# Mixed convolution weights and context terms: one product each, handed out by transfers through DRAM

## The chip, the cores and the metric

The kernel runs on one core of a Trainium2 chip. The metric is the device time of one execution in microseconds (us). An execution is timed as a whole; one execution was also recorded by the hardware profiler, and every row below is from that one.

## What is computed

Four layers follow one another on x of (32 batches, 64 channels, 1024). Each is x = x + FFN(cond(x)). Two kinds of conditioning matter here:

```python
# layers 0 and 3: a 1x1 convolution whose weights are mixed per batch
att   = softmax(mlp(cond))                          # (32, 8)
agg_w = einsum('bk,koi->boi', att, weight[..., 0])  # (32, 64, 64)
agg_b = att @ bias_k                                # (32, 64)
out   = einsum('boi,bih->boh', agg_w, x) + agg_b[:, :, None]

# layers 1 and 2: a grouped convolution, 9 taps, with a context term
out = conv(x, weight, groups=4)                     # (32, 64, 1024)
ctx = einsum('nd,od->no', cond, c_weight)           # (32, 64)
out = out + ctx[:, :, None] + fside[None, :, None]
```

The FFNs: layer 0 a top-1 mixture of LoRA experts, layer 1 a linear layer with weights and activations rounded to 8-bit integers and a separate part for outlier columns, layer 2 a linear layer plus top-2 LoRA experts, layer 3 a squared-relu FFN plus a latent expert and a layer norm.

## The kernel before

**Tiles.** x is kept on the chip as 16 tiles `x[j]` of 128 partitions: two batches of 64 channels, 1024 columns. So a mixed weight for tile j is a 128 x 128 matrix `aw[:, j, :]` with the 64 x 64 matrices of the tile's two batches on its diagonal and zeros elsewhere, and a context term for tile j is 2 x 64 numbers that every one of the 128 partitions needs.

**The mixing, for layers 0 and 3.** `fetch3` (L191) loads the eight weight matrices in four row groups. `mixing` (L195) clears `aw` on GpSimd (POOL), then makes 256 small products on TensorE (PE), L206: for each of 64 output channels, in four parts, and for both batches of a tile, an 8 x 64 slice of the weights is stationary and the 8 x 16 attention columns of all tiles move. VectorE (DVE) evicts with L212. Layer 0 does that at the start; layer 3's mixing stands in layer 2's loop, after tile 3's iteration (`if j == 4`, L802), and is stored to DRAM (`awd`) in two transfers; layer 3 loads four tiles' part at a time (`aw0` at L829 for the first, L865 for the later ones).

**The context, for layers 1 and 2.** `context` (L176) is called for each tile: POOL multiplies c_weight by the tile's two cond columns (`cpr`, L179), PE sums over partitions with a matrix of ones (`cb`, L186), and DVE adds `fside` (`cbs`, L188). `conv` (L233) then makes 32 products (L239) and DVE's eviction (L242) adds the context.

**Layer 0's loop** (L371 to L404) runs 16 + 5 iterations; in iteration `it` it loads two tiles ahead (`load`, L277: xT and x, on SyncE's queue, SP), a piece of layer 1's weight (`wt`), projects tile `it` (`z`, L286), makes the context of tile it-4, routes tile it-1 (`route0`: `lh`, L293 and L294, with the mixed weight `aw`), turns and multiplies tile it-2 (`whT` L316, `o` L325), and does layer 1's convolution of tile it-5 (`conv1`). When tile j's row is done, `by_rows` (L226) copies it from `x[j]` to `g`, rearranged for the convolution, in eight transfers on SP (L230); `g` has two buffers. Between these stand the steps of layer 1's weight quantization: its largest absolute values (`scb`, L342 and L344 on DVE, L396 on POOL with an all-reduce), the reciprocals (`top`, L399 to L401 on DVE) and the products (`wq`, L348 on POOL). After the loop, layer 1's `keep` (L408) starts; `bins<-zero` (L412) clears 8 MB of DRAM for layer 2's routing.

**Layer 2's first loop** runs over the 16 tiles: `features2` (context, convolution), `by_rows` two tiles ahead, half of an earlier tile's base product (`base2`, `o`, L681, stored by `x<-xo`, L689), `route2` (`lr`, L622), `place2` (`rk`, L653 and L654), and side work of layer 3's weights (`raw`, `ds`).

**Order.** Each engine runs its instructions in one order, fixed when the program is built: a scheduler orders each engine's instructions by its own estimate of when they can start, so the order differs from the text of the loops. SP, ACT and POOL issue transfers from their own queues; a transfer that waits holds back those behind it in its queue. Eight completion semaphores are shared by the transfers of SP and ACT, eight by POOL's: a transfer also waits for the one that used its semaphore last. Small row tiles (`tag="row"`) have 8 buffers, shared by contexts, biases and others.

## Time and profile before

| | us |
|---|---|
| runs, fastest, median, slowest of 3 | 1797.51, 1806.03, 1808.48 |
| profiled execution, its own time | 1798.23 |
| its span, first to last instruction | 1796.3 |

The mean TensorE clock granted in that execution is 0.984 of full speed. The span cuts into stretches at the places where the layers meet, with PE's busy time and DMA's mean share:

| stretch, us | what | PE busy | DMA share |
|---|---|---|---|
| 0 to 195.1 | layer 0 and layer 1's convolution | 163.4 | 0.75 |
| 195.1 to 365.7 | layer 1's FFN | 160.7 | 0.27 |
| 365.7 to 585 | layer 2, first loop | 212.6 | 0.56 |
| 585 to 763 | layer 2, experts | 171.3 | 0.81 |
| 763 to 1796.3 | layer 3 | 1015.4 | 0.57 |

How to read the rows. The page's first block gives each engine's busy time, share of the span and number of instructions. The chain is the work that ended last, followed back from the last instruction; its shares say where time, if taken away, would have to come from. A timeline row has the start, the duration, the engine, the line, the operation, destination<-source by the program's names, the shape, the count, and in brackets the idle time ahead of it and what ended that. In the table of stretches a row has the stretch, its length, and for PE, PEld, DVE, ACT and POOL the busy time with the number of instructions, then PE's granted clock, the DMA share and GB/s. A matrix product in f32 takes two passes and is counted as two instructions.

### The profile page before, as it was taken

To read this page: it belongs to the slowest core of one execution; us is meant where nothing else is said; L and a number is where in the kernel's file an instruction comes from. 1 tells how busy PE (TensorE), PEld (TensorE's weight loads), DVE (VectorE), ACT (ScalarE), POOL (GpSimd) and SP (SyncE) were. 2 spreads that over 40 slices of the span, in tenths; PEclk is the share of its full clock that TensorE was granted. 3 is DMA by queue.
4 is the path that set the end of the run, shared out by engine and by line. 5 is a ranking of instruction groups with operands and counts; after the bars stand their busy time and mean duration, and the time that the engine had idled before them with its cause. 6 is when DMAs were issued, how large, how long until landed. Compare 5 with 4: busy or idle time off the path is not lost.

```text
span 1796.3 us, 20943 instructions
## 1 busy us (share of the span) xinstructions
PE 1723.4 (96%) x7526; PEld 1157.7 (64%) x7526; DVE 811.5 (45%) x1700; ACT 203.4 (11%) x547; POOL 607.1 (34%) x628
## 2 busy tenths in 40 slices
PE   7987899999999999999999999999999999999997
PEld 6876577666766434486486585585584775774863
DVE  2889799455654433364152531143520333611224
ACT  1000344100000032010000010000010000000000
POOL 2347255522432564224044142052331242420231
PEclk9988899999999999999999999999999999999999
DMA  6886331277651499794576465475655574744423
GB/s 237 240 249 157 94 83 63 87 193 205 183 146 47 169 367 367 275 313 164 183 274 246 165 213 179 158 287 182 218 180 170 205 281 146 241 153 147 152 88 111
DMA packets 187351, 342.06 MB, mean 190 GB/s; under 512 B 20592, under 2 KB 93056, under 8 KB 187248
## 3 DMA queue, kind: packets, MB, share of 16 engines
q1 hardware_dynamic: 173152, 297.33, 51.2%
q0 software_dynamic: 14096, 43.39, 7.0%
q8 instruction: 60, 0.98, 0.2%
q14 instruction: 43, 0.35, 0.1%
HBM read 239.85 MB, written 83.89 MB: 180 GB/s over the span
## 4 chain that ended last, share of the span: by engine, by line
PE 79%; DMA 7%; POOL 4%; issue 4%; DVE 4%; SPq 2%; ACT 0%; POOLq 0%; DVEq 0%
PE p_d L1030 26%; PE p_u L975 25%; PE o L681 9%; PE conv L239 5%; PE oo L461 3%; DMA m<-outs,slot 2%; PE lr L622 2%; PE fold L263 1%; PE mix L565 1%; DMA bg<-in_b_dram,ewi 1%; POOL bin L537 1%; POOL x L470 1%; SPq L230 1%; DMA x<-in_x_dram 1%; POOL lo L454 1%
## 5 line engine op out<-in xcount | busy, mean ns | idle before, releaser
L1030 PE MATMUL p_d<-dn,h 128*128 128x512 f32 x1120 | 483.6, 593 | 0.0
L1030 PEld LDWEIGHTS p_d<-dn,h 128*128 128x128 f32 x1120 | 212.4, 190 | 263.9 <-issue 261.6
L975 PE MATMUL p_u<-y,up 128*128 128x256 f32 x1680 | 364.8, 379 | 0.5 <-DVE v_u L932 0.5
L975 PEld LDWEIGHTS p_u<-y,up 128*128 128x128 f32 x1680 | 318.8, 190 | 46.3 <-issue 2.1
L681 PE MATMUL o<-base,yT 128*128 128x512 f32 x512 | 225.1, 595 | 0.5 <-DVE eo L768 0.5
L681 PEld LDWEIGHTS o<-base,yT 128*128 128x128 f32 x512 | 95.3, 190 | 117.5 <-issue 113.8
L239 PE MATMUL conv<-cw,g 128*128 128x128 f32 x1024 | 126.0, 284 | 0.0
L239 PEld LDWEIGHTS conv<-cw,g 128*128 128x128 f32 x1024 | 123.6, 201 | 0.2
L461 PE MATMUL oo<-cbt,lo 128*128 128x512 f32 x256 | 104.2, 407 | 5.8 <-POOL lo L454 3.8
L461 PE MATMUL oo<-cbt,hi 128*128 128x512 f32 x256 | 104.7, 409 | 0.0
L988 POOL TENSOR_TENSOR raw<-u_u,v_u 128x256 f32<-128x256 f32 x40 | 30.2, 755 | 216.0 <-DVE v_u L932 215.9
L1003 POOL TENSOR_TENSOR h<-h 128x256 f32<-128x256 f32 x40 | 34.7, 869 | 148.4 <-DVE h L997 113.3
L687 DVE TENSOR_TENSOR xo<-x,o 128x256 f32<-128x256 f32 x64 | 35.4, 594 | 107.8 <-PE o L681 102.0
L932 DVE TENSOR_TENSOR v_d<-e_d,p_d 128x512 f32<-128x512 f32 x16 | 11.0, 687 | 143.4 <-PE p_d L1030 143.4
L975 PE MATMUL p_u<-y,s 128*128 128x256 f32 x320 | 72.2, 379 | 0.0
L932 DVE TENSOR_TENSOR v_u<-e_u,p_u 128x256 f32<-128x256 f32 x40 | 16.8, 420 | 111.5 <-PE p_u L975 111.5
L617 POOL TENSOR_TENSOR x<-x,bias 128x512 f32<-128x512 f32 x32 | 37.0, 1176 | 87.3 <-DMA g<-x 84.3
L975 PEld LDWEIGHTS p_u<-y,s 128*128 128x128 f32 x320 | 60.8, 190 | 8.3
L926 DVE TENSOR_TENSOR u_d<-e_d,p_d 128x512 f32<-128x512 f32 x16 | 11.0, 688 | 118.4 <-PE p_d L1030 118.4
L548 DVE TENSOR_TENSOR m<-m,m 128x1024 f32<-128x1024 f32 x32 | 42.4, 1326 | 45.2 <-DMA m<-outs,slot 23.0
L461 PEld LDWEIGHTS oo<-cbt,lo 128*128 128x128 f32 x256 | 49.0, 191 | 21.3 <-POOL lo L454 8.3
L975 PE MATMUL p_u<-y,r 128*128 128x256 f32 x240 | 57.7, 389 | 3.9 <-DVE v_u L932 2.8
(243 smaller groups left out, 2113.0 us busy)
## 6 DMA issues: line engine op xcount, KB each, us to landing
dn<-ds SPq DMA_DIRECT2D x160, 256.0 KB, 3.5
up<-us SPq DMA_DIRECT2D x60, 512.0 KB, 4.7
outs<-eo SPq DMA_DIRECT2D x48, 512.0 KB, 6.5
dn<-in_dn_dram SPq DMA_DIRECT2D x96, 256.0 KB, 3.5
g<-x SPq DMA_DIRECT2D x256, 64.5 KB, 2.5
up<-in_up_dram SPq DMA_DIRECT2D x30, 512.0 KB, 3.7
ds<-sum SPq DMA_DIRECT2D x20, 512.0 KB, 3.6
us<-s SPq DMA_DIRECT2D x20, 512.0 KB, 3.1
```

The costliest lines, as they stand in the source:

```text
L239: nc.tensor.matmul(ps[:, g, :], rows[:, 4 * b + g, ds(w, P)], cwt[:, g, w, :], start=(w == 0), stop=(w == 1))
L461: nc.tensor.matmul(po, terms[j][i][:, c, :], cbt[c][:, ts(n, HF)], start=(c == 0 and i == 0), stop=(c == NC - 1 and i == 1),)
L548: nc.vector.tensor_tensor(got[0], got[0], got[1 + k], ALU.add)
L617: nc.gpsimd.tensor_tensor(xh(j, h), xh(j, h), halved(bias2[:, ts(h, HF)]), ALU.add)
L622: nc.tensor.matmul(ps, yT[j][:, c, :], ra2[:, c, :], start=(c == 0), stop=(c == NC - 1))
L681: nc.tensor.matmul(po, yT[j][:, c, :], base[c][:, ts(n, HF)], start=(c == 0), stop=(c == NC - 1))
L687: nc.vector.tensor_tensor(new, old[:, ts(n, 64), :], add, ALU.add)
L932: nc.vector.tensor_tensor(m["v"], m["e5"], m["7"], ALU.add)
L975: nc.tensor.matmul(ps[0], ws[i][:, k, c, :], y[RHS[p]][:, c, :], start=(start and c == 0), stop=(c == 3), skip_group_check=not start,)
L988: nc.gpsimd.tensor_tensor(raw[:, 1, 1], m["u"], m["v"], ALU.add)
L1003: tt(h[:, 4], h[:, 1], h[:, 3], ALU.add)
L1030: nc.tensor.matmul(ps[q], hs[k][:, HLHS[p], ts(q, P)], ws[k], start=(start and k == 0), stop=(k == HG - 1), skip_group_check=not start,)
```

## The change

- `context`'s products are replaced by `contexts(n)`: one product of cond (stationary, all 32 batches) with c_weight for each of layers 1 and 2, `fside` added, stored to DRAM (`ctxd`). `context(n, j)` is now one SP transfer that loads tile j's 2 x 64 numbers to all 128 partitions.
- `mixing` is replaced by `aggregate(n)`: the attention is stationary in a 32 x 32 tile of the array, four such tiles on the diagonal hold the four row groups, and each takes 512 columns at a time: 8 products for a layer (16 in PE's passes). DVE evicts one half, ScalarE (ACT) the other, and ACT's queue stores the 32 mixed 64 x 64 matrices to DRAM (`aggd`) in four transfers of 128 KB. `spread` loads them back into the diagonal blocks of `aw`, which POOL has cleared, with two transfers of 256-byte runs: layer 0 all 16 tiles at once on ACT's queue, layer 3 four tiles at a time on SP's.
- Both layers' `aggregate` and both `contexts` stand at the start of layer 0. Layer 2's loop loses its mixing, and layer 3 keeps one cleared `aw3` for its later batches.
- Layer 0 loads three tiles ahead instead of two and projects one tile earlier; `z0` has 4 buffers instead of 3.
- Layer 0's order on SP changes with that: the loads of tiles 0 to 10 and six `wt` loads stand before the first `by_rows`, and `bins<-zero` stands ahead of the `by_rows` of tiles 7 and 8, where it stood after that of tile 9.
- The host lays the mixed weights out with the input channel first.

```diff
@@ -168,48 +168,47 @@
             nc.vector.tensor_copy(atT, ps)
             att[n] = atT
 
-    def context_weights(n, pool):
-        cw = pool.tile([P, 64], F32, name=f"ctxw{n}")
+    ctxd = {n: dram.tile([NB, 64], F32, name=f"ctxd_{n}") for n in (1, 2)}
+    aggd = {n: dram.tile([NB, 64, 64], F32, name=f"aggd_{n}") for n in (0, 3)}
+
+    def contexts(n, tmp):
+
+        cw = tmp(f"ctxw_{n}")[:, 0:64]
         nc.gpsimd.dma_start(out=cw, in_=a[f"cwT_{n}"])
-        return cw
-
-    def context(n, j, cw):
-
-        pr = small.tile([P, 2, 64], F32, tag="row", bufs=8, name=f"cpr{n}_{j}")
-        nc.gpsimd.tensor_tensor(
-            pr,
-            cw[:, None, :].to_broadcast([P, 2, 64]),
-            condT[:, ts(j, 2), None].to_broadcast([P, 2, 64]),
-            ALU.mult,
-        )
-        ps = bank(f"cb{n}_{j}", (P, 2, 64))
-        nc.tensor.matmul(ps, ones, pr, start=True, stop=True)
+        ps = bank(f"ctx_{n}", (NB, 64))
+        nc.tensor.matmul(ps, condT, cw, start=True, stop=True)
+        t = tmp(f"ctxs_{n}")[:NB, 0:64]
+        nc.vector.tensor_tensor(t, ps, fside[:NB], ALU.add)
+        nc.gpsimd.dma_start(out=ctxd[n], in_=t)
+
+    def context(n, j):
         cb = small.tile([P, 2, 64], F32, tag="row", bufs=8, name=f"cbs{n}_{j}")
-        nc.vector.tensor_tensor(cb, ps, fside[:, None, :].to_broadcast([P, 2, 64]), ALU.add)
+        nc.sync.dma_start(out=cb, in_=ctxd[n][ts(j, 2)].partition_broadcast(P))
         return cb
 
-    def fetch3(n, w3):
+    def aggregate(n, w3, t, evicts):
+
         for r in range(4):
             nc.gpsimd.dma_start(out=w3[ds(32 * r, KC)], in_=a[f"w3_{n}"][r])
-
-    def mixing(n, aw, w3, evict):
-
-        for t in aw:
-            nc.gpsimd.memset(t, 0.0)
-        w = w3.rearrange("k (o i) -> k o i", i=64)
-        at = att[n].rearrange("k (j h) -> k h j", h=2)
-        ps = [bank(f"awp_{n}_{r}", (P, 16, NT)) for r in range(4)]
-        for o in range(16):
+        ps = [bank(f"agg_{n}_{c}") for c in range(2)]
+        for c in range(2):
             for r in range(4):
-                q = ds(32 * r, KC)
-                for h in range(2):
-                    nc.tensor.matmul(ps[r][ds(64 * h, 64), o, :], w[q, o, :], at[q, h, :], start=True, stop=True)
+                q = ds(32 * r, 32)
+                k = ds(32 * r, KC)
+                nc.tensor.matmul(ps[c][q], att[n][k], w3[k, ts(c, HF)], start=True, stop=True)
+        for c in range(2):
+            evicts[c](t[:, ts(c, HF)], ps[c])
         for r in range(4):
-            for h in range(2):
-                q = ds(64 * h, 64)
-                m = NT // len(aw)
-                for i, t in enumerate(aw):
-                    evict(t[q, :, ds(64 * h + 16 * r, 16)], ps[r][q][:, :, ts(i, m)].rearrange("p o j -> p j o"))
+            nc.scalar.dma_start(
+                out=aggd[n][:, ts(r, 16), :].rearrange("b i o -> b (i o)"), in_=t[ds(32 * r, 32)]
+            )
+
+    def spread(n, aw, j0, eng):
+
+        src = aggd[n].rearrange("(j h) i o -> h i j o", h=2)
+        for h in range(2):
+            q = ds(64 * h, 64)
+            eng.dma_start(out=aw[q, :, q], in_=src[h, :, ds(j0, aw.shape[1]), :])
 
     def mixed_bias(n, j, bk, eng):
 
@@ -284,7 +283,7 @@
                 ps = bank(f"z0_{j}", (P, E0 + P))
                 for c in range(NC):
                     nc.tensor.matmul(ps, xT[:, c, :], ra[:, c, :], start=(c == 0), stop=(c == NC - 1))
-                z = lp.tile([P, E0 + P], F32, tag="z0", bufs=3, name=f"z0s_{j}")
+                z = lp.tile([P, E0 + P], F32, tag="z0", bufs=4, name=f"z0s_{j}")
                 nc.scalar.copy(z, ps)
                 zs[j] = z
 
@@ -350,12 +349,15 @@
                 nc.vector.tensor_scalar(q, t, ROUND, ROUND, ALU.add, ALU.subtract)
                 cbt.append(q)
 
-            xTs = {j: load(j) for j in range(2)}
+            xTs = {j: load(j) for j in range(3)}
             aw = lp.tile([P, NT, P], F32, name="aw_0")
-            w3 = slot_b("w3_0")
-            fetch3(0, w3)
-            mixing(0, [aw], w3, nc.vector.tensor_copy)
-            ctx1 = context_weights(1, lp)
+            nc.gpsimd.memset(aw, 0.0)
+            for n in (0, 3):
+                aggregate(n, slot_b(f"w3_{n}"), slot_b(f"agg_{n}"), (nc.vector.tensor_copy, nc.scalar.copy))
+                if n == 0:
+                    spread(0, aw, 0, nc.scalar)
+            for n in (1, 2):
+                contexts(n, slot_b)
             nc.gpsimd.dma_start(out=bw, in_=a["bw0"])
             nc.gpsimd.dma_start(out=cw1, in_=a["cw_1"])
             bias1 = lp.tile([P, D], F32, name="bias1")
@@ -367,19 +369,21 @@
             rsum = lp.tile([KC, E0 + P], F32, name="rsum_s")
             nc.vector.tensor_copy(rsum, ps)
 
+            project(0, xTs.pop(0))
             LATE = 5
             for it in range(NT + LATE):
-                if it + 2 < NT:
-                    xTs[it + 2] = load(it + 2)
+                if it + 3 < NT:
+                    xTs[it + 3] = load(it + 3)
                 if 2 <= it < 2 + NC:
                     w = wq.tile([P, D], F32, tag="w", name=f"wt_{it}")
                     nc.sync.dma_start(out=w, in_=a["w1T"][ts(it - 2, P), :])
                     wts.append(w)
+                if it + 1 < NT:
+                    project(it + 1, xTs.pop(it + 1))
                 if it < NT:
-                    project(it, xTs.pop(it))
                     bbs[it] = mixed_bias(0, it, bk, nc.gpsimd)
                 if 0 <= it - LATE + 1 < NT:
-                    cbs[it - LATE + 1] = context(1, it - LATE + 1, ctx1)
+                    cbs[it - LATE + 1] = context(1, it - LATE + 1)
                 if 0 <= it - 1 < NT:
                     route0(it - 1)
                 if 0 <= it - 2 < NT:
@@ -519,7 +523,6 @@
     x4 = [dram.tile([P, D], F32, name=f"x4_{j}") for j in range(NT)]
     usum = [dram.tile([P, 4, HF], F32, name=f"us_{g}") for g in range(NG)]
     dsum = [dram.tile([P, 4, HF], F32, name=f"ds_{g}") for g in range(NG)]
-    awd = dram.tile([P, NT, P], F32, name="awd")
     slot = cst.tile([P, 2, NT], I32, name="slot")
     bk3 = const("bk_3", a["bk_3"], (KC, 64))
 
@@ -593,7 +596,6 @@
         nc.sync.dma_start(out=half, in_=a["half"])
         part = lp.tile([P, 1], F32, name="part")
         nc.sync.dma_start(out=part, in_=a["part"])
-        cwt2 = context_weights(2, lp)
         base = []
         for c in range(NC):
             base.append(slot_a(f"base_{c}"))
@@ -612,7 +614,7 @@
             else:
                 t = wp.tile([P, D], F32, tag="bg", bufs=3, name=f"yT2_{j}")
             yT[j] = t.rearrange("p (c t) -> p c t", t=P)
-            conv(2, j, rows, cw2, context(2, j, cwt2), yT[j])
+            conv(2, j, rows, cw2, context(2, j), yT[j])
             for h in range(2):
                 nc.gpsimd.tensor_tensor(xh(j, h), xh(j, h), halved(bias2[:, ts(h, HF)]), ALU.add)
 
@@ -796,14 +798,6 @@
                 route2(j)
             if j >= 1:
                 place2(j - 1)
-            if j == 2:
-                w3 = w4("w3_3")
-                fetch3(3, w3)
-            if j == 4:
-                aw = [wp.tile([P, NT // 2, P], F32, tag="bg", bufs=3, name=f"aw3_{i}") for i in range(2)]
-                mixing(3, aw, w3, nc.vector.tensor_copy)
-                for i in range(2):
-                    nc.sync.dma_start(out=awd[:, ts(i, NT // 2), :], in_=aw[i])
             for r in waiting:
                 sums(*r)
             waiting = [raw(*todo.pop(0)) for _ in range(min(len(todo), 1 + j % 2))]
@@ -826,7 +820,8 @@
             if q % 3 == 2 and late:
                 base2(*late.pop(0))
         aw0 = slot_b("aw3_now")[:, : 4 * P].rearrange("p (t o) -> p t o", o=P)
-        nc.sync.dma_start(out=aw0, in_=awd[:, 0:4, :])
+        nc.gpsimd.memset(aw0, 0.0)
+        spread(3, aw0, 0, nc.sync)
         bbs = [mixed_bias(3, j, bk3, nc.gpsimd) for j in range(4)]
         got = [gather(j, slot_b) for j in range(2)]
         for j in range(AMID - 2, AMID):
@@ -859,12 +854,14 @@
         nc.sync.dma_start(out=t, in_=x4[j])
         return t
 
+    aw3 = lp.tile([P, 4, P], F32, name="aw3")
+    nc.gpsimd.memset(aw3, 0.0)
+
     def mixed(b):
 
-        aw = lp.tile([P, 4, P], F32, tag="aw", name=f"aw_{b}")
-        nc.sync.dma_start(out=aw, in_=awd[:, ts(b, 4), :])
+        spread(3, aw3, 4 * b, nc.sync)
         bbs = [mixed_bias(3, j, bk3, nc.gpsimd) for j in range(4 * b, 4 * b + 4)]
-        return blended(b, aw, lambda t: loaded(4 * b + t, "xm", 2), bbs)
+        return blended(b, aw3, lambda t: loaded(4 * b + t, "xm", 2), bbs)
 
     def gate(b, y):
 
@@ -1189,7 +1186,7 @@
             a[f"{k}_{n}"] = i[f"L{n}_cond_{k}"]
         for k in ("b0", "b1"):
             a[f"{k}_{n}"] = i[f"L{n}_cond_{k}"].reshape(P, 1)
-        a[f"w3_{n}"] = i[f"L{n}_cond_weight"].reshape(KC, 4, D).transpose(1, 0, 2)
+        a[f"w3_{n}"] = i[f"L{n}_cond_weight"].reshape(KC, 64, 64).transpose(0, 2, 1).reshape(KC, 4, D).transpose(1, 0, 2)
         a[f"bk_{n}"] = i[f"L{n}_cond_bias_k"]
     for n in (1, 2):
         a[f"cw_{n}"] = toeplitz(i[f"L{n}_cond_weight"])
```

## The prediction

> **What bounds the kernel now.** I read four views in turn. First the page: PE is busy 96% of the span, and the chain that ended last is 79% PE, so time taken off PE counts unless something else ends last there.
> ```profile
> span 1796.3 us, 20943 instructions
> PE 1723.4 (96%) x7526; PEld 1157.7 (64%) x7526; DVE 811.5 (45%) x1700; ACT 203.4 (11%) x547; POOL 607.1 (34%) x628
> PE 79%; DMA 7%; POOL 4%; issue 4%; DVE 4%; SPq 2%; ACT 0%; POOLq 0%; DVEq 0%
> ```
> Then the busy time by stretch, cut where the layers meet: only layer 0 is not PE's (163 of 195 us, DMA 0.75); layer 2's first loop is (213 of 219, DVE 118, POOL 71).
> ```profile
> 0.00:195.10 195.10, 163.44 (x1231) 138.63 (x1231) 139.87 (x265) 16.38 (x58) 87.38 (x99) 0.95 0.75 214
> 365.70:585.00 219.30, 212.63 (x1373) 151.11 (x1372) 117.68 (x496) 11.77 (x65) 70.64 (x75) 0.98 0.56 152
> ```
> Third, PE's timeline in layer 2 (start, duration, what): a regular iteration (cb, conv, o, lr, rk) and the mixing that stands ahead of tile 4's.
> ```profile
> 414.31 0.47 PE L186 MATMUL cb<-cpr,ones 128*128 128x128 f32 x2
> 414.62 3.74 PE L239 MATMUL conv<-cw,g 128*128 128x128 f32 x32
> 418.19 7.03 PE L681 MATMUL o<-base,yT 128*128 128x512 f32 x16
> 425.06 1.91 PE L622 MATMUL lr<-ra,yT 128*128 128x80 f32 x16
> 427.29 1.80 PE L206 MATMUL awp<-attT,w 8*64 8x16 f32 x169
> 433.15 1.47 PE L206 MATMUL awp<-attT,w 8*64 8x16 f32 x87 [4.06 <-issue]
> 434.56 0.80 PE L186 MATMUL cb<-cpr,ones 128*128 128x128 f32 x2
> 435.14 5.10 PE L239 MATMUL conv<-cw,g 128*128 128x128 f32 x32
> ```
> Fourth, layer 0. At the start PE does 13.2 us of mixing; in the middle it waits for the context's POOL product, which is itself stuck behind POOL and DVE work for the quantized weight (scb, top); and SP issues the 8 MB bins transfer between two tiles' loads.
> ```profile
> 13.89 13.18 PE L206 MATMUL awp<-attT,w 8*64 8x16 f32 x256
> 27.00 3.79 PE L366 MATMUL rsum<-ra,ones 128*8 128x136 f32 x16
> ...
> 35.14 0.49 PE L293 MATMUL lh<-rsum_s,bb 8*128 8x136 f32 x2
> ...
> 114.52 3.74 PE L239 MATMUL conv<-cw,g 128*128 128x128 f32 x32
> ...
> 128.57 0.80 PE L186 MATMUL cb<-cpr,ones 128*128 128x128 f32 x2 [6.74 <-POOL cpr L179]
> ```
> ```profile
> 127.72 5.50 DVE L399 TENSOR_SCALAR top<-top 128x256 f32<-128x256 f32 x2 [6.21 <-POOL scb L396]
> ```
> ```profile
> 118.29 5.05 SPq L230 DMA_DIRECT2D g<-x  x8
> 123.38 0.60 SPq L412 DMA_DIRECT2D bins<-zero  x1
> ```
>
> **The change, part by part.**
>
> *Layer 2, cb removed.* Its step on PE is 414.31 to 414.62: 0.30 us, 16 times = 4.8. PE is dense there, so all of it counts. POOL loses 16 x 0.40 (cpr) and DVE 16 x 0.28 (cbs); neither bounds.
>
> *Layer 2, mixing(3) removed.* From 427.29 (lr and rk done) to the end of tile 4's conv at 440.24; without mixing it would be 427.29 + 0.30 + 3.57 = 431.16. So 9.08 us: 7.3 are the products with the 4.06 us hole among them, 1.4 a conv that runs 5.10 instead of 3.74, 0.3 a slower cb. Lower bound 3.3 (1.80 + 1.47, if tile 4's conv would have waited out the hole anyway), upper bound the 9.1; I take 9.1, since the 8 loads of that tile's rows were issued from 419.93 to 425.61 and land 2.5 us later. Eight DVE evictions and two 512 KB stores go too, all beside PE.
>
> *Layer 2, context by transfer.* The new wait: DVE's conv eviction waits for an SP transfer of 64 KB (2 x 64 floats to 128 partitions). On SP it stands behind the tile's eight row loads (8 x 0.6 us), and behind it the ds/raw/x transfers, each 0.6 us later. It is issued about 5.8 us after the conv before; DVE needs it about 10.8 us after that conv, and PE needs the result only after the 6.9 us of o: 11.9 us from issue to harm. Nearest row: a g<-x, also 64 KB, lands 2.5 us (median) after issue. At that it costs nothing; the other end is g's longest, 13.5 (behind bins, in layer 0): 1.6 us x 16 = 26. I take nothing, the nearer row: layer 2's DMA share is 0.56 and it has no 8 MB transfer in that loop.
>
> *Layer 0, start.* Out go 256 products (13.2 us), in come 16 products of 512 columns. An o product of that width takes 0.43 us of PE per pass, two passes, so 0.86: 13.7 us one after another, 3.4 if four tiles of the array run together. Layer 0's eight decide: they wait for w3's last two loads, issued at 14.53 (POOL stands before them at a memset until 14.07) and, by the old mixing's unbroken run, landed by about 20 to 23. So the mixed weights are in SBUF at 22 to 27, stored at +4 to +5 (gd, 256 KB: 3.9; awd: 4.9), spread at +4 to +9 (2048 runs of 256 B; the bins transfer moved 16384 packets of 512 B in 26.0, so 3.3 by packets; x<-in_x took 9.2 in the crowded part): landed at 30 to 41. The two context products wait for cwT loads that queue on POOL behind others, so rsum, which PE issues after them, ends at 31 to 34, and then z0 to z2 (3 x 1.85, plus the ctx) run to about 40.8. The first lh, 35.1 before, comes at 40.8. From there to conv_0 the order holds four z (7.4), five lh pairs (4.3), three o (5.2) and four whT (0.4): 17.3 without waits, so conv_0 at 58.1, which was at 55.3: a loss of 3. Tile 0's rows stand on SP behind 22 tile loads and six wt (14.3 MB); the transfers' row for the first 60 us has up to 423 GB/s in a slice, so at some 410 these take 35 us from the first at 7.5 and are through before 47, when the row update lets tile 0's loads go. Bounds: nothing (the old order had 2 us of waits there, which may stay or go) and 11 lost, if the spread lands another 8 us after the 41.
>
> *Skill, first place.* The Trainium skill, "TensorEngine Tiling (Array Packing)", Restrictions and Gotchas, says that different row tiles cannot access one PSUM bank simultaneously; these four row tiles write one bank. By it the sum has 13.7, by full overlap 3.4. No row of this trace has such tiles. By either figure the sum stays, as rsum and z0 to z2 end later.
>
> *Skill, second place.* "DMA: Bandwidth & Descriptors", Specifications, asks for at least 512 B and says that less brings a read-modify-write; this speaks against 256-B runs. If that doubles the packet time, an estimate of 6.5 instead of 3.3 follows; no run here shows it yet.
>
> *Layer 0, middle.* cb and its wait for POOL go: an iteration from 8.33 to 8.03 us (0.3 x 7 = 2.1 before conv_7), and the stalls of 6.74, 7.00 and 3.35 us behind cpr lose their releaser. What is late next: DVE's top block (13 us, 127.7 to 140.8) still holds the evictions, POOL's wq products (two at 4.6 us) still hold the row updates, and the changed order issues bins before the row loads of tiles 7 and 8, where before it came after tile 9's. Behind bins a g landed in 13.5 us. With conv_6 at 106.6, bins is issued at about 100 and tile 7's rows land near 127: conv_7 at 128, which was at 114.5; conv_8 at 138 (130.9 before), conv_9 at 146.6 (149.1), and the end, by the wq products and the last row loads, at 192 instead of 195.1. A gain of 3 us. Bounds: +11 (no stall remains but POOL's) and -15 (bins, top block and late start one after another). I take 3, worked out step by step, though each step is an estimate.
>
> *Layer 3 start.* aw0's load (0.99 us on SP, 763.89) becomes a memset and two spread issues ahead of r<-in_up, which the chain runs through: one issue more, 0.6, and the wait for the memset: about 1 us lost (0.5 to 1.5). Its later spreads (256-B runs, 512 of them per batch) are needed some 250 us after issue: hidden, and if they were not, 4 x 5 = 20.
>
> *Sum.* 4.8 + 9.1 + 3 - 1 = 15.9. The profiled execution took 1798.2 (span 1796.3 and 1.9 around it): 1782.3. It lies 0.4% under the median of the runs, 1806.0, the three spanning 11; I put the forecast halfway, 1786.
>
> **Rivals.**
> - *Layer 0 gives more.* If the POOL stalls (17.4 us in all) go and bins covers nothing, 10 to 20 more: 1766 to 1776, say 1768. For: PE has 32 us idle there. Against: the DVE block and bins.
> - *Layer 0 eats it.* The start's chain through DRAM at its late end (41 + up to 8) and bins' stall in full: -11 to -15 instead of +3, so 1800 (1792 to 1812). For: DMA share 0.75 and the new order of bins.
> - *Slower: the context transfers land late in layer 2.* Up to 11.9 us they are free; each us above costs 16. At 12.9 the gain is gone, at 14.3 the kernel is 1% slower (1824), at 15 it takes 1836. For: the queue is shared with 512 KB transfers (raw, ds) on SP. Against: median 2.5 us of the same size in the same queue, and the chance of one late tile is not that of sixteen.
> - *Nothing comes of it:* PE is not the bound where the products go. Against: layer 2's 213 of 219. This is inside the second rival's time.
>
> **How the numbers follow.** A difference of about 1% (18 us) is what a measurement of this kernel can tell from none. Chances: forecast 0.48 (own range 1772 to 1800), layer 0 gives more 0.14, layer 0 eats it 0.22, slower by the transfers 0.16. The range 1760 to 1814 leaves out the last (0.16) and a rest of 0.03. Faster by over 1% means under 1788: 0.14 and 0.26 of the forecast's case = 0.40. Within 1%: 0.22 + 0.22 = 0.44. Slower: 0.16.
>
> **What would show it.** Layer 2's loop shorter by 14 us at equal iteration (12.6 instead of 12.9), with no idle before conv or lr and cbs landing in 2 to 4 us: the main term. PE idle before lr, released by DVE's yT, would be the slower rival. In layer 0: first lh near 41, a hole of some 13 us before conv_7 with g's landing over 20 us behind bins, and the layer's end near 192; no hole there speaks for the first rival, an end beyond 200 for the second. At layer 3's start, r<-in_up about 1 us later after the last of layer 2. The prediction is wrong if layer 2 does not give the 14, or if layer 0 moves by more than 10 either way.

## The result, and the profile after

The changed kernel took 1818.42 us (median of 14 runs, 1811.25 to 1830.49), the kernel before 1807.49 beside it (14 runs, 1797.51 to 1815.73). The ratio is 1.0068, 95% interval 1.0046 to 1.0090: 0.7% slower, some 11 us, where 1786 had been forecast and the range ended at 1814. The profiled execution of the changed kernel took 1824.41 us, that of before 1798.23. The pair differs by 26 us, because the one lies 6 above its median and the other 9 below. So stretches of single profiles are read here for where time went, and the ratios of many runs for how much.

First the page of the changed kernel. PE's busy time has not fallen (1723.4 before), although it has 540 instructions fewer, and DMA and DVE hold more of the chain. In layer 0 alone PE is busy for 168.1 us instead of 163.4, with 253 instructions fewer: the clock granted there is 0.91 of full speed instead of 0.95, and a convolution that follows a wait takes longer than the usual 3.74 us (6.17 at 149.24, below).
```profile
span 1822.6 us, 19874 instructions
...
PE 1723.9 (95%) x6986; PEld 1143.0 (63%) x6986; DVE 797.7 (44%) x1648; ACT 204.6 (11%) x549; POOL 589.6 (32%) x598
...
PE 76%; DMA 9%; DVE 6%; issue 4%; POOL 3%; SPq 2%; ACT 0%; ACTq 0%; POOLq 0%; DVEq 0%
```
Cut where the layers meet, at the start of `keep`, of layer 2's first convolution and of layer 3's first `p_u` product:

| stretch, us | before | after | forecast change | measured change |
|---|---|---|---|---|
| layer 0 and layer 1's convolution | 195.1 | 224.4 | -3 | +29.3 |
| layer 1's FFN | 170.8 | 171.5 | 0 | +0.7 |
| layer 2 | 405.2 | 391.4 | -13.9 | -13.8 |
| layer 3 | 1025.3 | 1035.3 | +1 | +10.0 |
| sum | 1796.3 | 1822.6 | -15.9 | +26.2 |

Layer 2 did what was forecast. In PE's timeline of the changed kernel an iteration runs from 418.09 to 430.76, 12.67 us instead of 12.90, and no row shows idle time in brackets; the mixing ahead of tile 4's convolution is gone:
```profile
418.09 3.82 PE L238 MATMUL conv<-cw,g 128*128 128x128 f32 x32
421.75 7.03 PE L683 MATMUL o<-base,yT 128*128 128x512 f32 x16
428.61 1.91 PE L624 MATMUL lr<-ra,yT 128*128 128x80 f32 x16
430.36 0.33 PE L655 MATMUL rk<-both,before 128*128 128x16 f32 x2
430.54 0.37 PE L656 MATMUL rk<-both,ones 128*128 128x16 f32 x2
430.76 3.82 PE L238 MATMUL conv<-cw,g 128*128 128x128 f32 x32
```
The view of the tile `cbs` of the changed kernel lists what its readers' engine waited for. The one wait for a context transfer, 13.8 us, lies in layer 0 (below); in layer 2 DVE has none. POOL's updates of x in layer 2 are put down to it five times, 36.1 us in all, but PE is busy there for 384.3 of 391.4 us. So the slower rival did not come.
```profile
  DMA cbs<-ctxd: 13.8, 1
```

Layer 0 lost the 29 us, in three places. **The start**, in PE's timeline of the changed kernel:
```profile
13.28 3.62 PE L198 MATMUL agg<-w,attT 8*32 8x512 f32 x4
19.54 5.58 PE L198 MATMUL agg<-w,attT 8*32 8x512 f32 x12 [2.64 <-DMA w<-in_w_dram]
...
44.23 0.47 PE L292 MATMUL lh<-rsum_s,bb 8*128 8x136 f32 x2
50.07 0.82 PE L293 MATMUL lh<-z0s,aw 128*128 128x136 f32 x2 [5.37 <-ACT z0s L287]
...
71.39 3.74 PE L238 MATMUL conv<-cw,g 128*128 128x128 f32 x32
```
The product with `aw` comes at 50.07 and conv_0, the convolution of tile 0, at 71.39 (55.3 before). PE names ACT's `z0s` as the releaser; ACT's timeline shows what stood ahead of that copy, and the chain of waits the two landings:
```profile
25.77 1.78 ACTq L202 DMA_DIRECT2D aggd<-agg  x4
35.13 1.44 ACTq L211 DMA_DIRECT2D aw<-aggd  x2
...
37.23 12.47 ACTq L202 DMA_DIRECT2D aggd<-agg  x4
49.74 0.62 ACT L287 COPY z0s<-z 128x136 f32<-128x136 f32 x3 [12.54 <-DMA aggd<-agg]
```
```profile
27.11 7.79 DMA aggd<-agg
35.82 13.43 DMA aw<-aggd
```
The stores take until 34.9 and the spread until 49.25; layer 3's stores, queued behind on ACT, keep the z copies back until 49.74. DMA's mean share is 1.03 from 26 to 35 us and 1.00 from 35 to 49.3. The queues' rows between 35.2 and 49.4 us (packets, MB, share of the 16 engines' time) say who had the engines:
```profile
q1 hardware_dynamic: 986, 3.57, 70.6%
q10 hardware_dynamic: 2142, 0.71, 28.3%
```
q1 carries SP's loads of tiles and weights, q10 ACT's spread and stores: 10.0 and 4.0 of the 14.2 us. The waiting went both ways: SP issued no load from 39.4 to 49.3, and 9.7 us of that are put down to the spread.

**The middle**, in the timelines of SP, DVE and PE of the changed kernel:
```profile
121.04 0.57 SPq L416 DMA_DIRECT2D bins<-zero  x1
123.41 32.20 SPq L229 DMA_DIRECT2D g<-x  x16
155.70 1.49 SPq L186 DMA_DIRECT2D cbs<-ctxd  x3
```
```profile
158.86 1.29 DVE L241 TENSOR_TENSOR y<-conv,cbs 128x512 f32<-128x512 f32 x2 [13.83 <-DMA cbs<-ctxd]
```
```profile
149.24 6.17 PE L238 MATMUL conv<-cw,g 128*128 128x128 f32 x32 [6.07 <-DMA g<-x]
```
Sixteen row loads, 0.6 us each elsewhere, take SP 32.2 us behind bins: the first of them stands for 22.50 us, the others take their 0.6. (In the kernel before, the first load behind bins, at 136.23, stood for 10.08 us.) conv_7 starts at 149.24 (114.5 before), after PE has idled for 12.85 us in all, 6.78 of them for DVE and 6.07 for the rows. Its eviction waits further, since its context transfer stands behind tile 8's rows on SP.

**The end.** POOL's updates of x wait for those same row loads, and its `wq` products, in one order with them, start at 165.61 instead of 140.93. Then POOL runs from 171.8 to 184.1 without a gap:
```profile
152.45 2.31 POOL L336 TENSOR_TENSOR x<-x,bias 128x512 f32<-128x512 f32 x2 [21.04 <-DMA g<-x]
...
165.61 4.66 POOL L347 TENSOR_TENSOR wq<-wt,top 128x1024 f32<-128x1024 f32 x2
...
172.64 1.17 POOL L336 TENSOR_TENSOR x<-x,bias 128x512 f32<-128x512 f32 x1
173.77 4.63 POOL L347 TENSOR_TENSOR wq<-wt,top 128x1024 f32<-128x1024 f32 x2
178.37 1.16 POOL L336 TENSOR_TENSOR x<-x,bias 128x512 f32<-128x512 f32 x1
179.50 4.63 POOL L347 TENSOR_TENSOR wq<-wt,top 128x1024 f32<-128x1024 f32 x2
```
In that time DVE stands in a maximum over 128x8, which takes 0.16 us where POOL is idle, and PE waits for DVE; the rows are DVE's and PE's:
```profile
161.91 0.16 DVE L333 TENSOR_TENSOR cmax<-cmax,cm 128x8 f32<-128x8 f32 x1
...
174.06 10.09 DVE L333 TENSOR_TENSOR cmax<-cmax,cm 128x8 f32<-128x8 f32 x1
```
```profile
184.90 0.79 PE L292 MATMUL lh<-rsum_s,bb 8*128 8x136 f32 x2 [9.58 <-DVE mx L297]
```

### The profile page after: what moved, and what is told of

The parts are those of the page before. It is cut to its first block, busy times and chain, and to the rows that moved or that the text cites. A ratio compares the mean times of both kernels' runs of the same rounds, so it can differ in the third digit from the quotient of the medians.

```text
span 1822.6 us, 19874 instructions
## 1 busy us (share of the span) xinstructions
PE 1723.9 (95%) x6986; PEld 1143.0 (63%) x6986; DVE 797.7 (44%) x1648; ACT 204.6 (11%) x549; POOL 589.6 (32%) x598
## 4 chain that ended last, share of the span: by engine, by line
PE 76%; DMA 9%; DVE 6%; issue 4%; POOL 3%; SPq 2%; ACT 0%; ACTq 0%; POOLq 0%; DVEq 0%
PE p_d L1027 26%; PE p_u L972 24%; PE o L683 9%; PE conv L238 4%; PE oo L465 4%; PE ex L767 2%; DMA m<-outs,slot 2%; PE lr L624 2%; SPq L229 1%; PE mix L568 1%; PE fold L262 1%; DMA m<-x 1%; POOL x L474 1%; POOL lo L458 1%; DMA wt<-in_w1T_dram 1%
## 5 line engine op out<-in xcount | busy, mean ns | idle before, releaser
L238 PE MATMUL conv<-cw,g 128*128 128x128 f32 x1024 | 130.9, 289 | 7.3 <-DMA g<-x 7.3
L336 POOL TENSOR_TENSOR x<-x,bias 128x512 f32<-128x512 f32 x32 | 37.6, 1193 | 87.4 <-DMA g<-x 28.1
L619 POOL TENSOR_TENSOR x<-x,bias 128x512 f32<-128x512 f32 x32 | 37.2, 1184 | 73.6 <-DMA cbs<-ctxd 36.1
## 6 DMA issues: line engine op xcount, KB each, us to landing
g<-x SPq DMA_DIRECT2D x256, 64.5 KB
```

What stands on the lines that cost most here:

```text
L238: nc.tensor.matmul(ps[:, g, :], rows[:, 4 * b + g, ds(w, P)], cwt[:, g, w, :], start=(w == 0), stop=(w == 1))
L336: nc.gpsimd.tensor_tensor(xh(j, h), xh(j, h), halved(bias1[:, ts(h, HF)]), ALU.add)
L619: nc.gpsimd.tensor_tensor(xh(j, h), xh(j, h), halved(bias2[:, ts(h, HF)]), ALU.add)
```

## The experiments

The first theory was that layer 0 loses by three things of its own: the weights' way through DRAM at the start, bins ahead of two tiles' rows, and the context transfers on SP. Its rivals: one of the three does it all, or the change of loads and buffers, or the place of the new DRAM buffers. Each ratio is to the kernel before, over many runs with its 95% interval; stage times are of one profile. Wherever the mixing is moved, the layout of `w3` on the host goes with it.

### The control

`before_again` is the kernel before, unchanged, once more.

> The kernel before once more, unchanged, for a second profile: its first profiled execution took 1798.2 us where its runs have a median of 1803 to 1807. Layer 0 (to keep) took 195.1, layer 2 405.2, layer 3 1025.3 in that profile. What differs by more than 2 us between the two profiles is the noise of a stage, against which the other comparisons are read. Expected: layer 2 and layer 1 within 2, layer 0 and layer 3 up to 6 longer.

One execution: 1798.71 us, span 1796.7; the stretches are 193.1, 169.7, 410.5 and 1023.4. So a stretch moves by 1 to 5 us by itself, and layer 2's gain lies between 14 and 19 by the choice of the profile.

### Bins

`after_bins` issues the clearing of bins in layer 1: its source is made by DVE from a result of layer 1's tile 3. `before_bins` does the same in the kernel before.
```diff
-            nc.sync.dma_start(out=bins..., in_=zero[:, None, :].to_broadcast(...))
...
+                if j == 3:
+                    nc.vector.tensor_scalar(zz, zero, rm, None, ALU.mult)
+                    nc.sync.dma_start(out=bins..., in_=zz[:, None, :].to_broadcast(...))
```

> The changed kernel with one edit: the 8 MB clearing of bins is made from a zero tile that depends on tile 3 of layer 1, so it cannot be issued in layer 0 any more. The changed kernel stands about 12 us over the one before in the runs (26 in the two profiled executions). Theory S (the start through DRAM is the whole loss; what follows would wait anyhow for POOL's and DVE's quantization work): the time moves by less than 5 us, conv_8 of layer 0 still starts near 145. Theory Q (bins on SP's queue holds the rows and context terms of tiles 7 to 9): conv_8 starts near 138, the 13.8 us wait of DVE for a context term is gone, and the time falls by 8 to 16 us, to between 4 us under and 4 us over the kernel before.

Measured: 1808.22 us, ratio 1.0031 (1.0013 to 1.0048). conv_7 starts at 137.5 instead of 149.2, `wq` at 151.5 instead of 165.6, and layer 0 ends at 207.5 instead of 224.4. DVE's wait of 13.8 us is gone. The gain over the changed kernel, some 7 us, lies between what the two theories had, and conv_8, at 147.6, fits neither.

> The kernel before with the same edit on bins alone: prices the place of bins without the change. Theory Q says the old place (behind the rows of tile 9) cost little, so within 4 us of the kernel before; if bins cost the old kernel too (its rows of tile 10 landed 13.5 us after issue), 4 to 10 us faster. If the clearing disturbs layer 1 instead (26 us of transfers among the weight loads), 2 to 8 us slower.

Measured: 1.0086 (1.0052 to 1.0121, four runs), 13 us slower, more than any of the three outcomes named; layer 0 ends at 200.9. So bins is not dear wherever it stands: held back, it gains 3.7 per mille in the new order and loses 8.6 in the old one.

### The mixing of layer 0

`after_mix0` keeps the old mixing for layer 0, on the chip; `after_mix0_bins` holds bins back as well.
```diff
-                aggregate(0, ...); spread(0, aw, 0, nc.scalar)
+            fetch3(0, w3)
+            mixing(0, [aw], w3, nc.vector.tensor_copy)
```

> The changed kernel with layer 0's mixed weights made as before, by 256 small products straight into the tile, with no way through DRAM; layer 3's are still made at the start and stored, the contexts go through DRAM. Theory S: first lh at 35 to 40 instead of 50, conv_0 at 55 to 60 instead of 71, and 10 to 15 us less in the end, so 0 to 4 us under the kernel before. Theory Q: the start comes earlier but the wait for bins and for the quantization swallows it: less than 5 us in the end.

Measured: 1.0039 (1.0015 to 1.0063), some 5 us less than the changed kernel, half of what theory S had at least; the first product with `aw` comes at 46.0, conv_0 at 65.8, and layer 0 ends at 214.9.

> Both edits. If start and bins are two losses of their own, the gains of the two single edits add up: some 20 to 28 us under the changed kernel, 8 to 16 under the kernel before, which is what layer 2 gives. If one hides the other, no more than the better single edit.

Measured: 1795.61 us, 0.9969 (0.9951 to 0.9986); conv_0 at 68.9, layer 0 ends at 202.8 in the profile, which is that of the slowest of ten runs. The two parts together are worth about 10 per mille, 3 and 4 each by itself.

`before_agg0` takes the other side: the kernel before with layer 0's mixing by `aggregate` and `spread`, and nothing else of the change.
```diff
-            fetch3(0, w3)
-            mixing(0, [aw], w3, nc.vector.tensor_copy)
+            nc.gpsimd.memset(aw, 0.0)
+            aggregate(0, slot_b("w3_0"), slot_b("agg_0"), (nc.vector.tensor_copy, nc.scalar.copy))
+            spread(0, aw, 0, nc.scalar)
```

> The kernel before with only layer 0's mixing by the 8 wide products, stores to DRAM and two spreading transfers on ACT's queue; contexts, prefetch, layers 2 and 3 are the old ones. If the way through DRAM costs by itself: lh with the mixed weight at 43 to 50 instead of 35.6, conv_0 6 to 12 us later, and 4 to 10 us more in the end. If the later waits of layer 0 swallow it: under 3 us.

Measured: 1836.61 us, 1.0177 (1.0144 to 1.0210): 32 us slower, more than the whole change, where 4 to 10 had been expected. conv_0 comes at 79.4. In PE's timeline:
```profile
32.92 3.62 PE L225 MATMUL agg<-w,attT 8*32 8x512 f32 x4
...
57.66 1.24 PE L320 MATMUL lh<-z0s,aw 128*128 128x136 f32 x4 [13.11 <-DMA aw<-aggd]
```
PE waits for the spread alone, but the spread starts late: PE's order here has `rsum` and some `z` products between the mixing products, the last of which end at 36.5 (at 25.1 in the changed kernel), and the spread is issued at 44.37 instead of 35.13. Then it lands in 12.50 us. SP's loads stand for ACT's transfers here too, 12.8 us for the stores and 11.2 for the spread, and from 32 to 39 us DMA's share is 0.01. So the 32 us are the price of the route with the order that it brings, not of the transfers alone.

### The products of layer 3 and of the contexts, later

`after_late3_bins` is `after_bins` with `contexts(1)`, `contexts(2)` and `aggregate(3)` in iterations 1, 2 and 3 of layer 0's loop. That takes layer 3's stores off ACT's queue at the start. `mix0_late3_bins` does it on `after_mix0_bins`.
```diff
+                if it in (1, 2):
+                    contexts(it, slot_b)
+                if it == 3:
+                    aggregate(3, slot_b("w3_3"), slot_b("agg_3"), (nc.vector.tensor_copy, nc.scalar.copy))
```

> As the changed kernel with bins held back (after_bins, 1.0031 of before), and now the products that layer 0 does not need at its start (both context products, layer 3's mixing with its four stores) are issued inside the loop, after iterations 1 to 3, instead of ahead of it. Theory A (the start is late because those stand ahead of layer 0's own work on PE and on ACT's queue, where the copies of z wait behind their stores): the first lh with the mixed weight comes at 40 to 44 instead of 50, conv_0 at 60 to 64 instead of 73, and 4 to 9 us are saved. Theory D (the way of layer 0's own weights through DRAM, stored at 26 to 35 and spread in 13 us, is what is late): lh stays at 47 or later, under 3 us saved.

Measured: 1.0053 (1.0035 to 1.0071). The first product with `aw` comes at 59.5 behind a wait of 12.59 us for the spread, conv_0 at 89.4, and 4 us are lost against `after_bins` where 4 to 9 had been hoped for. The queue on ACT is free of layer 3's stores, but the order on PE has changed as in `before_agg0`: the last mixing products start at 33.25, and the spread is issued at 46.48. So this run does not price the queue by itself. The rows of the changed kernel do: there the spread landed at 49.25, half a us before the z copies, so that without the queue the first product would have come less than 1 us earlier, an estimate from these two times.

> As after_mix0_bins (0.9969 of before; layer 0's mixing on the chip, bins held back), with the same products moved into the loop. Theory A: conv_0, which there stood at 69, comes to 56 to 60 as in the kernel before (55), and another 3 to 8 us go: 0.990 to 0.995. If the later part of layer 0 (quantization on POOL and DVE) sets its end whatever the start does: no change, 0.995 to 0.998.

Measured: 1.0027 (1.0005 to 1.0048); layer 0 ends at 214.9 instead of 202.8, although the first `lh` came at 38.4 instead of 47.4. It is 10 us slower than `after_mix0_bins`, where a gain of 3 to 8 or none had been expected. An early first product is not what makes the end early.

### Layers 2 and 3 alone

`before_l2_bins` is the kernel before with layer 2's contexts and layer 3's mixing changed, their products in iterations 2 and 3 of layer 0's loop, and bins held back. `l2_only` leaves layer 0 alone: the context product stands in layer 1 at tile 4, `aggregate(3)` where the old mixing was, and bins as before. `l2_best` loads the context weights earlier and makes the product at tile 6.
```diff
+                if j == 4:
+                    contexts(2, ...)
...
-            conv(2, j, rows, cw2, context(2, j, cwt2), yT[j])
+            conv(2, j, rows, cw2, context_d(2, j), yT[j])
...
-                mixing(3, aw, w3, nc.vector.tensor_copy)
-                for i in range(2):
-                    nc.sync.dma_start(out=awd[:, ts(i, NT // 2), :], in_=aw[i])
+                aggregate(3, w3, ..., (nc.vector.tensor_copy, nc.scalar.copy))
```

> The kernel before with only the part of the change that layer 2 and layer 3 see (layer 2's contexts by transfer, layer 3's mixing by the new products, made in layer 0's loop, its weights by 256-byte runs), and with bins held back to layer 1. Layer 0's mixing, contexts and prefetch are the old ones. Layer 2's gain of 12 to 14 us by the profile should stand alone, less what the products cost in layer 0 (some 4 us) and what layer 3 loses: 0.992 to 0.998. If layer 3's spread is what cost layer 3 its 4 to 10 us, those show here too.

Measured: 1.0009 (0.9989 to 1.0029), above the 0.992 to 0.998 expected. Layer 2 takes 391.8, but layer 0 ends at 205.4. Beside `before_bins` (1.0086), which holds bins back in the same way, it is 8 per mille or 14 us faster, about what layer 2 gains.

> The kernel before with the change in layers 2 and 3 alone, and nothing of it in layer 0: layer 2's context product is made in layer 1 (tile 4), its terms come by transfers; layer 3's mixing is made by the 16 wide products in layer 2's loop, where the 256 small ones stood, and stored by ACT's queue; layer 3 spreads it as in the changed kernel. If layer 0 is where the change loses and layer 2 where it wins: layer 0 at 195 to 200, layer 2 at 394 to 398 (4.8 for the context, some 5 of the 9 of the mixing), 6 to 10 us faster by the runs, 0.994 to 0.997. If what layer 2 wins is eaten by layer 3 (its spread, its loads): 0.998 to 1.001.

Measured: 1795.39 us, 0.9971 (0.9955 to 0.9988). The stretches are 192.5, 174.3, 395.1 and 1027.6. Layer 2's gain stands here by itself; of its 10 to 15 us some 5 remain over many runs, at the lower end of the 6 to 10 expected. Layer 1 takes some 4 us more (PE waits 4.0 us for the context's weights), and layer 3 2 to 4. PE's timeline has the eight products (in two passes) between two tiles:
```profile
425.73 1.92 PE L239 MATMUL agg<-w,attT 8*32 8x512 f32 x16
427.58 3.84 PE L279 MATMUL conv<-cw,g 128*128 128x128 f32 x32
```

> As l2_only (0.9971 of before, layer 1 174.3 us with a 4.0 us wait of PE for the context's weights), with those weights loaded at the start of layer 1 and multiplied two tiles later. The wait goes: another 3 to 4 us, 0.994 to 0.996. If the load is late for another reason (POOL's queue behind row updates), no change.

Measured: 0.9973 (0.9950 to 0.9996), no different from `l2_only`, where another 3 to 4 us had been hoped for. These two and `after_mix0_bins` are the versions that beat both kernels, the one before by about 5 us. `after_mix0_bins` still has the context transfers and the loads ahead, and stands where the part in layers 2 and 3 alone stands (0.9969 and 0.9971). So undoing the way through DRAM and the place of bins together takes away some 18 us, all or nearly all of layer 0's loss by the runs, and neither does so alone.

### Layer 1's contexts alone

`before_ctx1` is the kernel before with layer 1's contexts by one product and SP transfers; `before_ctx1_act` issues the transfers from ACT's queue.
```diff
-                    cbs[it - LATE + 1] = context(1, it - LATE + 1, ctx1)
+                    cbs[it - LATE + 1] = context_d(1, it - LATE + 1)
```

> The kernel before with only layer 1's context terms by one product and 16 SP transfers; layer 0's mixing, the prefetch, layers 2 and 3 are the old ones. If these transfers on SP (behind row loads, bins among them) are what holds DVE and POOL in layer 0's second half: 6 to 14 us slower. If they only take the place of POOL's product: within 4 us, or up to 8 faster, since PE's 17 us of waits for that product go.

> As before_ctx1 (the kernel before with layer 1's contexts by one product and 16 transfers; 1.0061 of before, layer 0 212.4 instead of 195.1), with the 16 transfers issued by ACT's queue instead of SP's. The order of the row loads on SP is then nearly that of the kernel before, with bins after the rows of tile 9. Theory P (what costs is their place in SP's queue, behind row loads that wait, and what they push back): layer 0 back to 193 to 199, the time within 4 us of the kernel before, or up to 8 faster as the waits for POOL's product are gone. Theory O (what costs is that without POOL's and PE's context work the rest of layer 0 runs in another order, loads of ew ahead of the last rows, row updates behind the quantization): layer 0 stays at 207 or later, 6 us or more over the kernel before.

Measured: 1.0061 (1.0039 to 1.0082) and 1.0063 (1.0043 to 1.0083); layer 0 ends at 212.4 and 210.6. So the transfers' place on SP is not the cause; the theory of the queue fell. What the rows show changed is the order of the rest, though no run tests that this order is the cause. In `before_ctx1` POOL makes two `wq` products in time, and the other six behind two tiles' updates:
```profile
144.49 4.65 POOL L364 TENSOR_TENSOR wq<-wt,top 128x1024 f32<-128x1024 f32 x2 [12.12 <-DVE mx L314]
155.19 2.31 POOL L353 TENSOR_TENSOR x<-x,bias 128x512 f32<-128x512 f32 x2 [6.05 <-DMA g<-x]
...
161.36 2.31 POOL L353 TENSOR_TENSOR x<-x,bias 128x512 f32<-128x512 f32 x2 [3.51 <-DMA g<-x]
...
163.99 4.64 POOL L364 TENSOR_TENSOR wq<-wt,top 128x1024 f32<-128x1024 f32 x2
```

### Loads, buffers and addresses

`after_noahead` goes back to two tiles loaded ahead, no early projection and three `z0` buffers; `after_noahead_ctx1` also to layer 1's old contexts. `after_addr` allocates the DRAM buffers of layer 1 to 3 ahead of the new ones.
```diff
-            xTs = {j: load(j) for j in range(3)}
+            xTs = {j: load(j) for j in range(2)}
...
-            project(0, xTs.pop(0))
...
-                if it + 1 < NT:
-                    project(it + 1, xTs.pop(it + 1))
                 if it < NT:
+                    project(it, xTs.pop(it))
```

> The changed kernel with the loads two tiles ahead and the projection in its own iteration, as before (three buffers of z). If the longer run of loads ahead of the first row loads is part of the loss: 3 to 8 us faster than the changed kernel (1.002 to 1.005 of before). If the start waits for the mixed weights anyhow: no change (1.005 to 1.009), and bins again ahead of the rows of tiles 7 to 9.

> As after_noahead (1.0084 of before, layer 0 228.2), with layer 1's contexts made as in the kernel before, by POOL, PE and DVE. If layer 1's context transfers are the greater part of the loss: 8 to 14 us less, 1.001 to 1.004 of before, layer 0 at 205 to 214. If the start is the greater part: under 5 us less.

> The changed kernel with only the order of its DRAM buffers altered: the new small buffers are allocated after the old ones, so those stand at the old places. Layer 3 took 1025.3 us in the profile before and 1035.3 after, with the loads of xm at 4.2 us instead of 3.3. Theory M (where the buffers lie sets how fast layer 3's tiles load): layer 3 back to 1025 to 1028, xm at 3.3. Theory R (the difference is that of one execution from another, or comes from the spread): 1029 to 1036 again. The time as a whole within 5 us of the changed kernel's by R, 5 to 10 us less by M.

Measured: 1.0084 (1.0056 to 1.0112), 1.0070 (1.0048 to 1.0092) and 1.0073 (1.0048 to 1.0097), none told apart from the changed kernel's 1.0068. In the profile of `after_noahead` conv_0 comes at 78.3 instead of 71.4, and layer 0 ends 4 us later: loading and projecting ahead softens the start. `after_noahead_ctx1` was to be 8 to 14 us faster than `after_noahead` if layer 1's contexts were the greater part of the loss; by the ratios it is 2 to 3 us faster, within the intervals. So in the new order they are not, though alone in the old one they cost 11. Layer 3 takes 1027.2, 1029.2 and 1027.7 us there, with the same code in which the changed kernel's profile shows 1035.3. So most of the 10 us in that row of the table is the scatter of one execution; addresses are no cause. Some of it stays: the fourteen profiles with the changed layer 3 have 1027 to 1035 us there, 1030.5 on average, the six with the old one 1023 to 1031, 1026.1 on average. That is some 4 us.

### Moving the quantization by itself

In the eighteen profiles up to here layer 0 ended 21 to 29 us after POOL's last `wq` product, whatever the variant. That led to a second theory: the quantization sets the end. `after_wqfirst` and `l2_best_wqfirst` force the `wq` products ahead of the updates of tiles 3 to 11, since the updates' operand is written again (with the same values) after the last product.
```diff
+                if c == NC - 1:
+                    nc.vector.scalar_tensor_tensor(bias1, t, 0.0, bias1, ALU.mult, ALU.add)
+                    for j in range(3, 12):
+                        biased(j)
```

> The changed kernel with one difference in GpSimd's order: layer 1's row updates (x + bias1) of tiles 3 to 11 can no longer stand ahead of the wq products, since bias1 is first rewritten (with the same values) after the last wq. No wq product then waits behind an update that waits for a g transfer. In sixteen profiles layer 0's end followed the last wq product by 21 to 29 us. If the quantization sets layer 0's end: the wq products start right after top (all-reduce at about 112, top some 25 later, so about 140 instead of 165.6), end by about 175 instead of 200, and layer 0 ends at 200 to 205 instead of 224.4; over many runs 8 to 15 us less than the changed kernel, ratio to before 0.998 to 1.003. If the quantization is only carried along and SyncE's late row loads (bins, 32 us) set the end: wq ends early all the same, but layer 0 still ends at 218 to 226 and the ratio stays at 1.005 to 1.009.

> The version with the layer 2 and 3 part alone, with the same forced order (row updates of tiles 3 to 11 after the wq products). There the wq products stand at 139.6 to 171.8 and layer 0 ends at 192.6. If the quantization sets the end: wq ends some 5 to 10 us earlier (by 163 to 167), layer 0 ends at 183 to 188, ratio to before 0.992 to 0.995. If not: layer 0 ends at 190 to 195 and the ratio stays at 0.997 to 0.998.

Measured: 1.0083 (1.0055 to 1.0112) and 1.0036 (1.0015 to 1.0057). In `after_wqfirst` the products start at 153.5, not at the 140 expected, and end at 182.3 instead of 200.1, and layer 0 still ends at 224.2. So the theory falls as it was put. The reason given for the other outcome, late row loads, does not hold either: PE's conv_15 starts at 201.91 instead of 216.97. What ate those 15 us is in DVE's timeline, beside POOL's deferred updates in one unbroken run to 222.0:
```profile
204.51 0.69 DVE L241 TENSOR_TENSOR y<-conv,cbs 128x512 f32<-128x512 f32 x1 [1.02 <-PE conv L238]
205.12 16.93 DVE L333 TENSOR_TENSOR cmax<-cmax,cm 128x8 f32<-128x8 f32 x1
```
```profile
195.84 26.18 POOL L340 TENSOR_TENSOR x<-x,bias 128x512 f32<-128x512 f32 x23
```
In `l2_best_wqfirst` the products end at 159.2 instead of 171.8, but POOL then works off 25 us of updates before it makes the context product of a late tile, PE waits 20.73 us for that, and layer 0 ends at 204.7 instead of 192.6.

## Why the prediction was wrong

The sum had +3 us for layer 0, and the profiled pair lost 29.3 there; that is the term that failed, and it passes the 10 us that the prediction itself had named as its sign of being wrong.

- **Layer 2, cb and mixing: right.** 13.9 forecast, 13.8 in the profiled pair. That the two agree so closely is luck: the eleven profiles with all of the change in layer 2 have 389 to 398 us there (392.6 on average), the three that make layer 3's products in layer 2 395 to 401, and the six with the old layer 2 405 to 411 (408.5 on average).
- **Layer 2, context by transfer at no cost: right.** DVE, which reads it, did not wait there.
- **Layer 0, start: wrong in size, and the first step that failed.** The weights were to land at 30 to 41; they landed at 49.25, at the end of the bound. The products were ready as forecast (the first store is issued at 25.77, forecast 22 to 27). The stores took 9 us instead of 4 to 5, and the spread 13.4 instead of 4 to 9; conv_0 came 13.3 us after its forecast. What was priced too low is the overlap of the stores and the spread with the tile loads. The rows taken as prices, gd at 3.9 and awd at 4.9, stand in layers with a DMA share of 0.27 to 0.56, but this chain stands where it is 1.0. Four stores of the same size landed in 2.0 us (median) in `after_late3_bins`, where DMA's share from 32 to 39 us is 0.00, in 4.2 in `before_l2_bins` at a share of 0.76, and the last of them took 7.79 in the changed kernel at 1.03. The spread's own packets were priced about right: 28.0% of the 16 engines' time from 44.4 to 57.6 us in `before_agg0`, or 3.7 us, where 3.3 had been weighed, while SP's loads had 64.5%, or 8.5 us. That SP's loads would in turn stand for ACT's transfers was not in the step either: they were to be through before 47 and are issued until 55.4. Tile 0's row loads, at 62.92, did not wait for that, since its row update ends at 62.89.
- **Layer 0, middle, bins: right in kind.** From bins to conv_7 28.2 us, forecast 28 (100 to 128), with 12.85 us of idle PE, forecast some 13. But it began 21 us later than forecast, 13.3 of them from the start.
- **Layer 0, middle, the gain of 3: wrong in sign.** From conv_7 to the end 75.2 us, forecast 64. The cb waits on PE did go. What came instead was POOL's order: `wq` 25 us late, then an unbroken run of it in which DVE stood for 10.09 us and PE for 9.58. The longest such maximum in the profile of before is 1.68 us, and the step priced POOL's products by POOL's time only.
- **Layer 3: its start about right, the whole too small.** The row loads are issued 2.7 us after the last `x<-xo`, 2.0 before (at 781.54 and 764.97); PE did not wait for them. But the layer as a whole lost some 4 us on average, where 1 was forecast; what it loses them by stays open.
- **The rivals.** Layer 0 ate it: -11 to -15 had been priced and 29 came in the profile; the median, 1818, lies above that rival's 1812. The late transfers in layer 2 and the larger gain did not come.
- **The two figures from pages.** The Trainium skill, "TensorEngine Tiling (Array Packing)", Restrictions and Gotchas, has different row tiles not access one PSUM bank at a time. In `l2_only` sixteen such products took 1.92 us, 0.12 each, where an `o` product of the same width takes 0.44: in this arrangement the four tiles overlap, against the rule. In layer 0 the same sixteen took 9.2 us in the order in which their weights landed, without harm. The Trainium skill, "DMA: Bandwidth & Descriptors", Specifications, has 512 bytes as the least transfer for line rate and a read-modify-write below it. From that an estimate of 6.5 us had been set beside the 3.3 for the 2048 runs of 256 bytes. The 3.7 us in `before_agg0` show no doubling; the landing took 13.43 us in the changed kernel and 12.50 there, with the tile loads on the same engines.

What stays open: the parts do not add. In the old order the route alone costs 32 us and layer 1's contexts alone 11, and both with layer 2's gain cost 11 in all. The profiles show a loop in which the rows, POOL's updates, the `wq` products and DVE wait for one another, and every edit tried changed where the waits fall. That undoing the route and the place of bins together takes away some 18 us is shown; how these divide between the two is not. The runs show that no single one of them sets the end; they do not show what a given edit will cost. A version of `after_wqfirst` with the updates spread out was not tried; by its rows it would end layer 0 near 209, an estimate from conv_15's last product at 207.1 and the 2.2 us from the last eviction to `keep`.

## What to carry to other kernels

Price a transfer by rows from the stretch in which it will stand: the same stores and spreads that nobody waits for in layers 2 and 3 cost 23 us on the way of the first product, where the tile loads fill the DMA engines. A product that leaves PE is a gain only where PE is dense; in a stretch where four engines wait for one another, first ask which in-order queue the removed waits may have kept in step. When parts of a change sit in stretches with different limits, try each alone: the part in layers 2 and 3 alone is 0.3% faster, the whole 0.7% slower.

## What was not expected of the hardware

DVE can stand while POOL works without a gap, and not for one instruction only. The 128x8 maximum took 10.09 us across five POOL instructions and 16.93 across the rest of 23, ending with POOL's run both times, and 0.16 where POOL was idle. Evictions, which read one operand from PSUM, took 0.68 us beside the same POOL run. The Trainium skill, "SBUF — State Buffer", section "SBUF: two separate sides", says that a DVE operation with two SBUF inputs and a GpSimd operation that reads SBUF lock shared ports against each other, for a whole instruction. These rows agree that it is such an operation that is held; that it can be held over a whole run of instructions, the page does not say. Nor does it have to be: beside POOL's run of 22 updates in `l2_best_wqfirst` (167.06 to 192.03) two such maxima took 0.41 and 0.17 us. What decides between the two is not shown.
